# Running sums kept by columns in the scan turns by columns of a two-layer scan, attention and experts kernel

## The chip, the cores and the metric

The kernel runs on one core of one Trainium2 chip. A core has five engines, each with a queue of its own that is worked through in order: PE (TensorE, matrix products), DVE (VectorE), ACT (ScalarE), POOL (GpSimd) and SP (SyncE, which here starts nearly all transfers). PE's weight loads are shown as an engine of their own, PEld. The metric is the device time of one execution in microseconds (us); lower is better.

## What is computed

The input `x` is 4 images of 384 channels and 32 x 32 places, all in float32. Layer 0 normalizes it by groups and runs a selective scan over the 1024 places of each image in four directions `k`: by rows, by columns, and both of these backwards. Layer 1 is attention with a causal window of 64 and six heads, and then a mixture of four experts of which each token uses two. Cut to what the change touches:

```python
def _cross_scan(x):
    x0 = x.reshape(B, D, H * W)
    x1 = jnp.transpose(x, (0, 1, 3, 2)).reshape(B, D, H * W)
    return jnp.stack([x0, x1, x0[..., ::-1], x1[..., ::-1]], axis=1)
...
def step(h, inp):
    dtt, ut, bt, ct = inp
    dA = jnp.exp(dtt[..., None] * A)
    h = h * dA + (dtt * ut)[..., None] * bt[:, :, None, :]
    y = jnp.einsum('bkdn,bkn->bkd', h, ct)
    return (h, y)
...
ys = ys + Ds.reshape(K, D)[None, :, :, None] * u
...
y0 = ys[:, 0]
y2 = ys[:, 2][..., ::-1]
yt = ys[:, 1] + ys[:, 3][..., ::-1]
yt = jnp.transpose(yt.reshape(B, D, W, H), (0, 1, 3, 2)).reshape(B, D, L)
return y0 + y2 + yt
```

The state has 16 numbers for each channel and place; `y` sums over them. The results of the four directions and the term with `Ds` are added up place by place, and directions 1 and 3 come by columns and have to be turned for that.

## The kernel before

**How the order comes about.** The kernel's parts are generators. A recorder, `Machine` (line 213), runs them all against a model of the core: each step asks for one operation or, through `Engine.all` (144), for several at once; `Engine.ask` (155) gives it a price; `account` (264) adds the price to the engine's clock; `choose` (324) takes the one that can start first, moved by a bias. The experts have the bias `LATER`, +6 us, and most other parts `EARLY`, -6 us. The instructions go out in the order so found, on each engine. Prices are thus no times of the chip, but they set the order on all five queues. For a product on PE whose output has 32 partitions the price is that of line 180, and line 197 marks it as `steady`, which `account` (275) reads: other products take 1.9 times their price when the model thinks PE's clock is low, a steady one doesn't. `work` (198) is what the model counts as PE's activity for that.

**The scan.** A turn is one image `b` and one direction `k`; `ORDER` (538) puts the directions by columns, 1 and 3, ahead of 0 and 2, so turns 0, 1, 4, 5, 8, 9, 12 and 13 of the 16 go by columns. In a turn there are 12 blocks of 32 channels, and for each block four slots of four states; one slot fills a tile of 128 partitions (32 channels x 4 states) by 1024 places. For every slot:
- POOL multiplies the spread input by the spread `B` into a tile `z` (`times_b`, 801); there are seven tiles `z`.
- ACT makes the decay `dA` in PSUM (`decay`, 817); there are two of these.
- DVE scans (`scan`, 843), and POOL or DVE multiplies by the spread `C` (`times_c`, 830).
- PE adds the states up (`fold_y`, 873). Two blocks go together. Each of the two tiles `z` of a step is multiplied by `fold`, a 128 x 32 matrix that adds four partitions each, once for each half of the image's 32 rows. The four products write four groups of 32 partitions of one PSUM bank `ps`, 512 places wide. After four steps the bank holds the sums over all states, 16 products in all.

The sums over the directions run through memory. `normal` (659) writes `dsum` times the normalized input, `yd`, to `ydr`, as two halves of 512 places for each channel. `fold_y` loads the sums so far into `prev`, starts the bank with the product `ident` x `prev`, lets the sixteen products add to it, copies the bank back over `prev` on ACT (901) and stores it. Layer 1 reads `ydr` when an image is done, in `tile` (965). In all turns `ydr` lies by rows. A tile `z` of a turn by columns has its 1024 places as 32 columns of 32 rows, so its half is read as 16 rows by 32 columns, with steps of 32 elements:

```python
if k % 2:
    rhs = z.rearrange("p (w h) -> p h w", h=HH)[:, ts(h, HH // 2), :]
else:
    rhs = z[:, ts(h, LH)]
```

**Beside and after the scan.** `layer1` (1431) takes up an image when its four turns are done: attention in `tokens` (946), the choice of experts in `route` (1189). `experts` (1297) works on 19 blocks of 128 tokens for each image. For one block there are eight weight tiles of 576 KB, 36 products for the hidden layer (`ps_hid`, bank to `gelus` on ACT) and 12 for the output (`y_ff`). `combine` (1389) puts the results together. So layer 1 of one image runs beside the scan of the next ones, and that of the last image and what is left of the others comes after the last scan. ACT changes its function table (`ACT_TABLE_LOAD`) when it goes from the exponential to Gelu, to the logarithm or back.

Of the kernel before, what the change touches and what calls it, by code (L numbers as in the profile page):

```python
# [12 lines left out]
AF = mybir.ActivationFunctionType  # L13
# [5 lines left out]
B, D, HH, WW = 4, 384, 32, 32  # L19
# [52 lines left out]
class Stock:  # L72


    def __init__(self, m, pool, tag, n, shape):
        self.m, self.free = m, []
        self.tags, self.queue = {}, []
        self.add(pool, tag, n, shape)
# [32 lines left out]
class Op:  # L111


    def __init__(self, eng, outs, ins, cost, table, size):
        self.eng, self.outs, self.ins, self.cost, self.table, self.size = eng, outs, ins, cost, table, size
        self.work = 0.0
        self.steady = False


TABLES = {AF.Exp: "exp", AF.Ln: "ln", AF.Gelu: "gelu", AF.Sqrt: "sqrt"}  # L120
# [10 lines left out]
class Engine:  # L131
# [12 lines left out]
    def all(self, calls):  # L144

        asked = [self.ask(*c) for c in calls]
        outs, ins = ([ap for o in asked for ap in getattr(o, side)] for side in ("outs", "ins"))
        whole = Op(self.name, outs, ins, sum(o.cost for o in asked), None, 0)
        whole.work = sum(o.work for o in asked)
        whole.steady = asked[-1].steady  # L150
        yield whole
        for op, a, k in calls:
            getattr(self.real, op)(*a, **k)  # L153

    def ask(self, op, a, k):
        aps = [v for v in list(a) + [v for n, v in k.items() if n not in ("out", "accum_out")] if hasattr(v, "tensor")]
        if "out" in k:
            outs, ins = [k["out"]], aps
        else:
            outs, ins = aps[:1], aps[1:]  # L160
        if op == "value_load":
            outs, ins = [], aps
        if op == "tensor_tensor_reduce":
            outs, ins = outs + ins[-1:], ins[:-1]
        if k.get("accum_out") is not None:
            outs = outs + [k["accum_out"]]
        for v in list(k.values()):
            if isinstance(v, bass.IndirectOffsetOnAxis):
                ins = ins + [v.ap]
        n = max(v.free_size() if callable(v.free_size) else v.free_size for v in (outs if op == "matmul" else outs + ins))  # L170
        size, table = 0, None
        if "dma" in op:
            size = max(_nbytes(v) for v in outs + ins[:1])
            if op == "indirect_dma_start":
                size = P * D * 4
            cost = dict(pool=1.0, act=0.38, sp=0.48)[self.name]
        elif self.name == "pe":
            cost = max(n, 90) * (0.00088 if op == "transpose" else 0.00176)
            if outs[0].shape[0] == 32:
                cost = 0.108 + 0.000417 * n  # L180
            if ins[0].shape[0] < 32:
                cost *= 0.6
        elif self.name == "act":
            cost = 0.08 + 0.00085 * n + 0.1 * sum(hasattr(k.get(v), "tensor") for v in ("bias", "scale"))
            cost += 0.19 if "accum_out" in k else 0.0
            table = TABLES.get(a[2]) if op == "activation" else None
        elif self.name == "pool":
            cost = 0.1 + 0.0022 * n
        elif self.name == "sp":
            cost = 1.5  # L190
        else:
            cost = 0.17 + 0.00198 * n if "scan" in op else 0.14 + 0.00105 * n
            if n < 256 and not any(v.space == PSUM for v in outs + ins):
                cost += 0.5
        asked = Op(self.name, outs, ins, cost, table, size)
        if self.name == "pe":
            asked.steady = outs[0].shape[0] == 32
            asked.work = cost * min(ins[0].shape[0], P) / P if outs[0].shape[0] > 32 else 0.5 * cost
        return asked


def _nbytes(ap):
    n = 4
    for s in ap.shape:
        n *= s
    return n
# [6 lines left out]
class Machine:  # L213
# [50 lines left out]
    def account(self, op, start):  # L264
        e = op.eng
        if op.table and op.table != self.table:
            start += TABLE_LOAD
            self.table = op.table
        end = start + op.cost
        if e == "pe":  # L270

            left, end = op.cost, start
            while left > 0:
                n = int(end / WINDOW)
                f = 1.0 if op.steady or self.worked.get(n - 1, 0.0) > WINDOW / 3 else COLD
                step = min(left * f, (n + 1) * WINDOW - end + 1e-6)
                self.worked[n] = self.worked.get(n, 0.0) + op.work * step / f / op.cost
                left, end = left - step / f, end + step
        self.busy[e] += end - max(self.clock[e], start)
        self.clock[e] = end  # L280
        if op.size:
            self.dma = max(self.dma, end) + op.size / DMA_RATE
            end = max(end + DMA_TIME, self.dma + 1.0)
            e = "dma"
        for aps, log, w in ((op.ins, self.read, False), (op.outs, self.written, True)):
            for ap in aps:
                name = ap.tensor.name
                if str(ap.space) .endswith("DRAM"):
                    self.dram.setdefault(name, []).append((*self.span(ap), end, w))
                elif log.get(name, (0.0, None))[0] <= end:  # L290
                    log[name] = end, e
        self.reach = max(self.reach, end)
# [80 lines left out]
WINDOW, COLD = 3.413, 1.9  # L373
# [5 lines left out]
def conv_attn_hybrid(  # L379
# [35 lines left out]
    dsum = const.tile([P, T], F32, name="dsum")  # L415
# [58 lines left out]
    with tc.tile_pool(name="setup", bufs=1) as setup:  # L474
# [15 lines left out]
        for j in range(JB):  # L490
            ps = banks.now("ps_al")
# [44 lines left out]
    pwl = dram.tile([P, T * D], F32, name="pwl", bufs=1)  # L536

    ORDER = (1, 3, 0, 2)
    turns = [(b, ORDER[ki]) for b in range(B) for ki in range(KG)]
    blocks = [(i, t, j) for i in range(len(turns)) for t in range(T) for j in range(JB)]  # L540
    NSLOT = len(blocks) * NG
# [7 lines left out]
    pe, act, dve, pool, sp = m.pe, m.act, m.dve, m.pool, m.sp  # L549
# [65 lines left out]
    def group_norm(b):  # L615
# [21 lines left out]
        ps = yield from banks.take("ps_gm", 0)  # L637
# [21 lines left out]
        def normal(t):  # L659
            u = yield from us_.take("un")  # L660
            yield from sp.dma_start(u, x[b, ts(t, P)].rearrange("p h w -> p (h w)"))
            yield from act.activation(
                u, u, AF.Identity, bias=g_off[:, t : t + 1], scale=g_rstd[:, t : t + 1]
            )
            yield from sp.dma_start(udr[b][t], u)
            yd = yield from zs_.take("yd")
            yield from act.activation(yd, u, AF.Copy, scale=dsum[:, t : t + 1])
            us_.give(u)
            for j in range(JB):
                yield from sp.dma_start(  # L670
                    ydr[b][t, j].rearrange("(q d) l -> d q l", q=2),
                    yd[32 * j : 32 * j + 32, :].rearrange("d (q l) -> d q l", q=2),
                )
            zs_.give(yd)

        yield from m.together([normal(t) for t in range(T)], T if b == 0 else 1, EARLY)
        have.add(("u", b))

# [194 lines left out]
    def fold_y(n):  # L873


        i, t, j = blocks[n]
        b, k = turns[i]
        rows_y = ydr[b][t, j : j + 2].rearrange("j r l -> (j r) l")
        prev = yield from yps.take("yp")
        yield from sp.dma_start(prev, rows_y)  # L880
        ps = None
        for g in range(NG):
            s = n // 2 * SP + 2 * g
            yield lambda: s in ready and s + 1 in ready
            pair = zs[s], zs[s + 1]
            yield m.settled(*pair)
            mm = Calls()
            if ps is None:
                ps = yield from banks.take("ps_y", 0)
                mm.matmul(ps, ident, prev, start=True, stop=False)  # L890
            for n_z, z in enumerate(pair):
                for h in range(2):
                    if k % 2:
                        rhs = z.rearrange("p (w h) -> p h w", h=HH)[:, ts(h, HH // 2), :]
                    else:
                        rhs = z[:, ts(h, LH)]
                    q = 32 * (2 * n_z + h)
                    mm.matmul(ps[q : q + 32, :], fold, rhs, start=False, stop=g == NG - 1)
            yield from pe.all(mm)
            zs_.give(zs.pop(s), zs.pop(s + 1))  # L900
        yield from act.copy(prev, ps)
        banks.give(ps)
        yield from sp.dma_start(rows_y, prev)
        yps.give(prev)
        folded[b] = folded.get(b, 0) + 2
        if folded[b] == KG * NB:
            have.add(("scan", b))
# [601 lines left out]
```

## Time and profile before

| | before |
|---|---|
| median of 3 runs | 4246.56 us (4246.25 to 4254.88) |
| profiled execution, its own time | 4255.8 us |
| its span, first to last instruction | 4254.0 us |
| mean granted clock of PE | 0.819 |
| PE, PEld busy | 3377.0, 1952.7 us |
| DVE, ACT, POOL busy | 2852.8, 2373.1, 2813.7 us |
| `ps_y<-z,fold` on PE | 3072 records, 827.1 us busy |
| first and last of them | 112.6 and 3174.1 us |
| function table loads on ACT | 340 and 1 at the start, 1283 ns each |
| scan of the last turn's end to the end of all | 1079 us |

Busy time counts overlapping records once. A float32 product leaves two records on PE, so 3072 records are 1536 products. A record's length is not what a product costs when others run beside it: the four products of a step write different groups of partitions and overlap. What one costs is read from when the next starts. PE's granted clock is shown as a share of full speed. The turns start at about 113, 278, 441, 621 us (image 0), 776, 989, 1194, 1404 (image 1), 1590, 1777, 1985, 2190 (image 2) and 2397, 2599, 2794, 2992 us (image 3).

### The profile page before, as it was taken

The page shows a single profiled execution, that of the slowest core. Times are in us where ns is not written, and L with a number is a line of the kernel's source. Part 1 is how long each engine was busy: PE and PEld are TensorE (multiplying, and loading weights), DVE is VectorE, ACT ScalarE, POOL GpSimd, SP SyncE. Part 2 cuts the span into 40 slices and gives each one's busy share as a digit, 9 for nine tenths or more (in the row PEclk, how much of TensorE's full clock was granted, in tenths as well). Part 3 has the DMA queues.
Part 4 walks back from the last instruction along what each step waited for, and adds up shares of the span by engine and source line. Part 5 has one row for each costly group of instructions (what it writes and reads, how often), then busy time and mean ns, then how long its engine had stood idle before and what let it go on. Part 6 is the DMA issues. An engine that isn't in the chain of part 4 may idle for free. (4 is left out here: it accounts for less than half of the span.)

```text
span 4254.0 us, 50073 instructions
## 1 busy us (share of the span) xinstructions
PE 3377.0 (79%) x16222; PEld 1952.7 (46%) x16222; DVE 2852.8 (67%) x2995; ACT 2373.1 (56%) x3961; POOL 2813.7 (66%) x1468
## 2 busy tenths in 40 slices
PE   2556555588875987978788787887899999999997
PEld 1000110144441553534445343444567777887875
DVE  2999999987888978888888888888861222001001
ACT  2555455666655887777677767677663443222221
POOL 1999989997897899988878889898871001101001
PEclk7655665687875998878788887887899999999997
DMA  6566563542446985635668846556577438998995
GB/s 210 200 239 230 202 227 127 177 150 107 150 145 240 365 326 189 221 124 195 211 232 293 297 149 205 187 189 216 176 248 260 138 103 301 355 319 294 313 319 165
DMA packets 368573, 935.16 MB, mean 220 GB/s; under 512 B 48372, under 2 KB 160120, under 8 KB 368312
## 3 DMA queue, kind: packets, MB, share of 16 engines
q1 hardware_dynamic: 360120, 906.79, 61.3%
q0 software_dynamic: 8192, 25.17, 1.7%
q8 instruction: 129, 2.11, 0.2%
q14 instruction: 132, 1.08, 0.1%
HBM read 786.39 MB, written 164.30 MB: 223 GB/s over the span
## 5 line engine op out<-in xcount | busy, mean ns | idle before, releaser
L142 POOL TENSOR_TENSOR z<-dts,bc 128x1024 f32<-128x1024 f32 x768 | 1796.2, 2364 | 236.5 <-PE ps_y L153 136.9
L142 ACT ACTIVATE dA<-dts,a 128x1024 f32<-128x1024 f32 x768 | 853.1, 1118 | 488.6 <-DVE z L142 467.6
L153 PE MATMUL ps_y<-z,fold 128*32 128x512 f32 x3072 | 827.1, 914 | 320.8 <-DVE z L142 162.8
L142 DVE TENSOR_TENSOR_SCAN dA<-dA,z 128x1024 f32<-128x1024 f32 x414 | 947.3, 2288 | 111.1 <-ACT dA L142 92.1
L142 POOL TENSOR_TENSOR z<-z,bc 128x1024 f32<-128x1024 f32 x354 | 831.1, 2360 | 101.0 <-DVE z L142 100.1
L142 DVE TENSOR_TENSOR_SCAN z<-dA,z 128x1024 f32<-128x1024 f32 x354 | 795.7, 2276 | 55.7 <-ACT dA L142 53.1
L153 PEld LDWEIGHTS ps_hid<-xbt,w_sb 128*128 128x128 f32 x5472 | 683.4, 201 | 136.5 <-issue 22.4
L153 PE MATMUL ps_hid<-xbt,w_sb 128*128 128x128 f32 x5472 | 702.0, 286 | 40.7 <-ACT dt L142 16.4
L153 PE MATMUL y_ff<-w_sb,hs 128*128 128x384 f32 x1824 | 664.4, 503 | 14.3 <-ACT hs L142 7.9
L142 ACT ACTIVATE hs<-ps_hid,bb 128x128 f32<-128x128 f32 x912 | 271.9, 366 | 542.2 <-PE ps_hid L153 417.3
L142 DVE TENSOR_TENSOR z<-dA,bc 128x1024 f32<-128x1024 f32 x414 | 505.9, 1222 | 23.3 <-PE ps_y L153 0.5
L153 PEld LDWEIGHTS ps_y<-z,fold 128*32 128x32 f32 x3072 | 93.9, 122 | 800.7 <-POOL z L142 336.5
L142 ACT ACT_TABLE_LOAD x340 | 436.2, 1283 | 12.0 <-PE ps_g L153 5.8
L153 PEld LDWEIGHTS y_ff<-w_sb,hs 128*128 128x128 f32 x1824 | 333.4, 196 | 228.0 <-issue 40.3
L142 POOL DMA_INDIRECT cb<-ysdr,idx x64 | 61.8, 966 | 548.8 <-DMA cb<-t2dr 269.7
L153 POOL TENSOR_TENSOR rn<-rn,half 128x1 f32<-128x1 f32 x96 | 52.6, 548 | 288.6 <-DVE rn L153 286.6
L142 DVE COPY xbt<-ps_xb 128x384 f32<-128x384 f32 x40 | 22.2, 556 | 329.2 <-PE ps_xb L153 329.2
L153 PE MATMUL ps_y<-yp,ident 128*128 128x512 f32 x192 | 139.1, 814 | 90.0 <-ACT yp L142 20.9
L142 POOL DMA_INDIRECT xsdr<-tks,idx x64 | 63.7, 995 | 208.5 <-DMA xsdr<-tks,idx 151.3
L153 PE MATMUL ps_o<-v,pt 128*128 128x64 f32 x720 | 160.1, 345 | 6.1 <-ACT dt L142 2.3
L142 DVE COPY yb<-y_ff 128x384 f32<-128x384 f32 x27 | 15.0, 556 | 214.4 <-PE y_ff L153 205.1
L153 PEld LDWEIGHTS ps_o<-v,pt 128*128 128x128 f32 x720 | 130.1, 228 | 43.7 <-ACT dt L142 4.0
(187 smaller groups left out, 3480.3 us busy)
## 6 DMA issues: line engine op xcount, KB each, us to landing
w_sb<-wl SPq DMA_DIRECT2D x608, 576.0 KB
dts<-dtr SPq DMA_DIRECT2D x384, 512.0 KB
bc<-xdr SPq DMA_DIRECT2D x128, 512.0 KB
ub<-udr SPq DMA_DIRECT2D x48, 512.0 KB
dtr<-e SPq DMA_DIRECT2D x48, 512.0 KB
dtr<-dt SPq DMA_DIRECT2D x48, 512.0 KB
yp<-ydr SPq DMA_DIRECT2D x96, 256.0 KB
ydr<-yp SPq DMA_DIRECT2D x96, 256.0 KB
```

Of the source, the lines that this page charges most:

```text
L142: return getattr(self.real, op)(*a, **k)
L153: getattr(self.real, op)(*a, **k)
```

## The change

The sums in `ydr` lie by columns while the two turns by columns of an image run, and by rows from then on. `yd` is written in that layout (each half as 32 columns of 16 rows), so ACT reads `u` with steps of 32 elements. In the turns by columns PE reads the half of `z` as 32 columns of 16 rows, each column a run of 16 elements. In the second of these turns, direction 3, ACT's copy of the bank writes `prev` by rows, with steps of 32 elements. Sizes, products and transfers stay what they are.

Three things in the recorder change too. The price of a product with 32 output partitions goes from 0.108 + 0.000417 n to 0.01 + 0.00022 n. The mark `steady` is gone, so such a product too takes 1.9 times its price where the model thinks the clock is low. `Engine.all` hands on the function table of its operations.

```diff
@@ Engine.all
-        whole = Op(self.name, outs, ins, sum(o.cost for o in asked), None, 0)
+        table = next((o.table for o in asked if o.table), None)
+        whole = Op(self.name, outs, ins, sum(o.cost for o in asked), table, 0)
         whole.work = sum(o.work for o in asked)
-        whole.steady = asked[-1].steady
@@ Engine.ask
             if outs[0].shape[0] == 32:
-                cost = 0.108 + 0.000417 * n
+                cost = 0.01 + 0.00022 * n
...
         if self.name == "pe":
-            asked.steady = outs[0].shape[0] == 32
             asked.work = cost * min(ins[0].shape[0], P) / P if outs[0].shape[0] > 32 else 0.5 * cost
@@ Machine.account
-                f = 1.0 if op.steady or self.worked.get(n - 1, 0.0) > WINDOW / 3 else COLD
+                f = 1.0 if self.worked.get(n - 1, 0.0) > WINDOW / 3 else COLD
@@ conv_attn_hybrid
     ORDER = (1, 3, 0, 2)
+    LAST_BY_COLUMNS = 3
@@ normal
-            yield from act.activation(yd, u, AF.Copy, scale=dsum[:, t : t + 1])
+            yield from act.activation(
+                yd.rearrange("p (q w h) -> p q w h", q=2, w=WW),
+                u.rearrange("p (q h w) -> p q w h", q=2, w=WW), AF.Copy, scale=dsum[:, t : t + 1],
+            )
@@ fold_y
                     if k % 2:
-                        rhs = z.rearrange("p (w h) -> p h w", h=HH)[:, ts(h, HH // 2), :]
+                        rhs = z.rearrange("p (w h) -> p w h", h=HH)[:, :, ts(h, HH // 2)]
...
-        yield from act.copy(prev, ps)
+        if k == LAST_BY_COLUMNS:
+            yield from act.copy(
+                prev.rearrange("p (h w) -> p w h", w=WW), ps.rearrange("p (w h) -> p w h", w=WW)
+            )
+        else:
+            yield from act.copy(prev, ps)
```

## The prediction

> **What bounds the kernel now.** I read the page's busy shares, then windows on the work's stages, then PE's timeline, and the waits last. PE is busiest over the whole span, but that average mixes two stages: the scans end at 3174.6 us (last `ps_y<-z,fold`), and from there PE does little but the experts' two products. In the windows view (columns: stretch, length, busy us of PE, PEld, DVE, ACT and POOL, with counts, granted clock, DMA share, GB/s):
>
> ```profile
> 113.00:278.00 165.00, 97.22 (x234) 14.23 (x230) 159.38 (x107) 88.08 (x99) 154.70 (x68) 0.62 0.62 222
> 800.00:3175.00 2375.00, 1916.31 (x9013) 1060.01 (x9009) 2001.59 (x2024) 1678.29 (x2631) 2062.04 (x1038) 0.82 0.59 206
> 3175.00:4254.00 1079.00, 1037.97 (x6185) 819.79 (x6183) 150.69 (x464) 298.06 (x883) 91.51 (x126) 0.95 0.76 258
> ```
>
> The first scan turn is DVE's: 159 of 165 us busy, PE 97. From 800 us nothing is full (POOL 87%, DVE 84%, PE 81%, ACT 71%): the in-order queues wait on one another. The tail is PE's, 1038 of 1079 us. So time goes where PE has to do expert work after the last scan, and what PE does earlier shortens the tail. The tail's rate is in one undisturbed block of experts (four chunks of hidden and output products and one turn of the input):
>
> ```profile
> 3640.33:3656.44 16.11, 16.11 (x101) 12.93 (x100) 1.11 (x2) 3.53 (x12) 2.91 (x3) 1.00 1.03 403
> ```
>
> Now the sums that the change touches. First records in turn 5 (by columns, reading every 32nd element), then turn 7 (by rows), both at full clock, from PE's timeline:
>
> ```profile
> 989.47 1.90 PE L153 MATMUL ps_y<-z,fold 128*32 128x512 f32 x8
> 991.30 0.55 PE L153 MATMUL ps_g<-ident,yl 128*128 128x128 f32 x3
> ...
> 1434.46 1.92 PE L153 MATMUL ps_y<-z,fold 128*32 128x512 f32 x16
> 1436.31 0.59 PE L153 MATMUL y_ff<-w_sb,hs 128*128 128x384 f32 x1
> ```
>
> A group of four matmuls leaves 8 records (3072 for 1536 in the program). By columns one group holds PE until the next product starts, 991.30 - 989.47 = 1.83 us; by rows two take 1436.31 - 1434.46 = 1.85, so 0.93 each. The same by tile (min/median/max ns, whole turns 4 and 5, then 7):
>
> ```profile
> L153 PE MATMUL ps_y<-z,fold x384: 1024/1035/1206, 776.1 to 1185.3; 128*32 128x512 f32 x192
> ...
> L153 PE MATMUL ps_y<-z,fold x192: 592/593/1060, 1404.4 to 1579.7; 128*32 128x512 f32 x192
> ```
>
> At the low clock both take the same: in turn 3, by rows, half groups (the two matmuls of one `z`) take 1.92 us, as in turn 0, by columns:
>
> ```profile
> 645.50 1.92 PE L153 MATMUL ps_y<-z,fold 128*32 128x512 f32 x4 [1.79 <-DVE z L142]
> ...
> 264.39 1.92 PE L153 MATMUL ps_y<-z,fold 128*32 128x512 f32 x4 [2.69 <-POOL z L142]
> ```
>
> So a better read is worth about 0.9 us a group, and only at full clock.
>
> **What the Trainium skill says.** "SBUF — State Buffer", Specifications (TRN2): lines are 16 bytes, full bandwidth wants at least two hits on each, and each crossing pays. Elements 128 bytes apart hit a line once; the trace agrees (1035 against 593 ns). Runs of 16 f32 hit each line four times: by the page they read at full rate. No record of the kernel before shows such runs. "Advanced Engine Details and Errata", PSUM Cachelines, is gloomier: any access that isn't contiguous slows matmuls, though it then asks only for pairs; the output here stays contiguous. "TensorE: Matmul & The Clock Gate", What's actually happening: the clock is half or full, nothing between; so a mean clock c means a share 2c - 1 at full. The records' two levels, 593 and 1060, agree.
>
> **The change part by part.**
>
> *The read.* Only the turns by columns change. Turns 0 and 1 are DVE's and mostly at low clock: worth nothing, since DVE hides it. In turns 4, 5, 8, 9, 12, 13 the windows give clocks 0.74, 0.82, 0.87, 0.81, 0.81, 0.79; the shares at full clock are 0.48, 0.64, 0.74, 0.62, 0.62, 0.58, mean 0.61. Of 6 x 24 = 144 groups 88 gain 1.83 - 0.93 = 0.90 us: 79 us of PE. Bounds: 0 (the runs read like single elements) and 0.90 x 144 = 130 (all at full clock). I take the row rate, for the reason of the line size.
>
> *The recorder.* It writes the order on all engines by its own prices. A group of four at n = 512 was charged 4 x (0.108 + 0.2135) = 1.286 at any clock; now 4 x 0.1226 = 0.49, or 0.93 where it believes the clock low. (The table that `all` now hands on is always empty: only PE, DVE and POOL use `all`.) The program of after has the same work, moved: all four turns of batch 0 still hold no expert product on PE, and before the last `ps_y<-z,fold` stand 1,224 hidden matmuls in place of 1,017 and 399 output matmuls in place of 333. A block has 36 and 12: 207/36 = 5.75 and 66/12 = 5.5, so 5.6 blocks leave the tail, 5.6 x 16.11 = 90 us off it. That counts wholly, because PE is 96% busy there. The attention matmuls stand on the same side as before (432 `ps_qk` before the last fold in both).
>
> *What it costs in the scans.* PE gets 90 us more and 79 less: +11, at its busy share there (1916/2375 = 0.81) 14 us. If the queues absorb it in the 459 us PE now idles, 0; I take 14.
>
> *ACT.* In the order of turns 4 to 15, 316 table loads stand where 289 did: 27 x 1.283 (`ACT_TABLE_LOAD`) = 35 us. The copies that turn the sums (24) write every 32nd element; the nearest row is `xo<-ps_x`, 582 ns straight and 1119 at most with such a write: 24 x 0.54 = 13 us. Of the 12 `yd` copies, now read with such a step and in batches 1 to 3 nine, between 0 and 9 x 1.1 = 10 us (doubling 1143 ns). Some 57 us of ACT beside 697 us idle. DVE waited on ACT's `dA` 89.2 + 53.1 = 142 us in this stretch, so part arrives: a quarter, 15 us (0 to 57). The bank that a turned copy holds 0.5 us longer and the 3 `yd` copies before the first scan stay under 5 us in all and are inside this.
>
> *SP and DMA.* Counts are equal. The weights of 5.6 blocks (8 x 576 KB each, 26 MB) start in the scans: over 2375 us 11 GB/s on 206, hidden by a DMA share of 0.59. In turn 7, at 0.91 already, 27 more hidden matmuls are 0.75 block, 3.5 MB, at 403 GB/s 9 us if nothing hides it. I take 0. `dts` loads are queued on the same SP behind the weights; that is what would be late.
>
> Sum: -90 + 14 + 15 = -61 us. Against its own execution (4255.8, span 4254.0) 4195; on the median 4246.56, 4185.
>
> **Rivals.**
>
> *Runs of 16 read no faster (slower).* Place: the 88 groups at full clock. Then PE gets 90 us unpaid, 90/0.81 = 111 in the scans; and each group, charged 0.49 against 1.83, is 1.34 late where it was 0.55: 88 x 0.79 = 70, of which half passes to ACT and DVE, 35. -90 + 111 + 35 + 15 = +71: 4318. For it: the second page. Against: the line size. Between the two ends the result falls 132 us over 0.90 us, so 61 are used up 0.42 us above the row rate: it decides from about 1.35 us a group on.
>
> *The plan promises too much (no change).* The charge was near the mean (1.286 against 0.93 and 1.9), now it is half of either. In the six row turns clocks of 0.68, 0.93, 0.81, 0.89, 0.81, 0.88 give 96 groups at full clock and 48 at low: lateness before 48 x 0.63 = 30, after 96 x 0.44 + 48 x 0.99 = 90, so +60; by columns about +11. If all of these 71 us reach the scans: -61 + 71 = +10, 4257. For it: nothing on ACT can overtake a copy that waits for PE. Against: PE waits for `z` far more than `z` for PE: 336.5 + 317.9 us of its weight loads' waits, 137.1 the other way, so most lateness falls into gaps.
>
> *The scans get shorter too.* POOL waited on `ps_y` 24.1, 17.5 and 25.0 us in the three stretches by columns, and DVE 63.0 + 35.1 on `ps_o` and `ps_s` from 800 us on. Half of the first and a third of the second are 66: 4119. Against: row turns, with a fast sum, take as long (1189 us for six, 1210 by columns).
>
> **How the numbers follow.** The forecast, 4185, has 0.50, its own range 4130 to 4235 (0 or 57 on ACT, 9 on DMA, PE's saving up to 130). The shorter scans have 0.18, the overfull plan 0.15, the slow read 0.12, and 0.05 is for what I don't see in a new order on five queues, slower. The range 4105 to 4270 leaves out the slow read, half of the last and a little at the low end. 0.2% is 8.5 us, about the spread of the three runs and what can be told from no change. Faster: 0.50 + 0.18 and a third of 0.15, less a little, 0.72. Same: a third of 0.15, 0.06. Slower: the rest, 0.22.
>
> **What would show it.** A median near 593 ns for the folds in turn 8 shows the read right; 1035 shows it wrong. The last fold near 3174.6 + 29 and a tail near 990 us confirm the split; a tail 90 us shorter with a last fold past 3260 speaks for the overfull plan, with more waits of POOL and ACT on `ps_y`. The turned copies near 1.1 us and 363 table loads beside 340 show ACT's part. I am wrong if the tail keeps its 1079 us: then PE was not what it was made of.

## The result, and the profile after

| | before | after |
|---|---|---|
| median | 4250.72 us (4 runs, 4246.25 to 4264.91) | 4206.01 us (4 runs, 4193.36 to 4210.73) |
| ratio to before, 95% interval | | 0.9885 (0.985 to 0.9919) |
| span of the profiled execution | 4254.0 us | 4209.0 us |
| last fold starts (the 3174.1 given above is its weight load) | 3174.6 us | 3219.4 us |
| from there to the end | 1079 us | 990 us |
| PE busy | 3377.0 us | 3272.0 us |

The change makes the kernel faster by 1.15%. The split matters more than the sum: the tail is 90 us shorter and the scans are 45 us longer. The windows view of after, on the stretches that answer to those of before (columns: stretch, length, busy us of PE, PEld, DVE, ACT and POOL with counts, granted clock, DMA share, GB/s):

```profile
113.00:283.00 170.00, 93.13 (x236) 16.39 (x234) 163.20 (x109) 90.80 (x102) 161.01 (x72) 0.61 0.63 222
800.00:3221.00 2421.00, 1919.30 (x9574) 1132.96 (x9571) 2013.82 (x2051) 1749.33 (x2718) 2061.45 (x1045) 0.82 0.62 216
3221.00:4209.00 988.00, 949.89 (x5625) 751.86 (x5623) 139.83 (x442) 275.88 (x822) 85.06 (x118) 0.94 0.73 250
```

The first turn is DVE's as before. In the middle stretch PE has as much busy time as before (1919 against 1916 us) and has done 560 records more: what the folds gave up, expert products took. ACT is 71 us busier. The tail is still PE's, 96% busy.

The fold itself, from PE's timeline in turn 8, by columns, at full clock:

```profile
1612.31 1.06 PE L152 MATMUL ps_y<-z,fold 128*32 128x512 f32 x8
1613.31 2.27 PE L152 MATMUL ps_hid<-xbt,w_sb 128*128 128x128 f32 x18
```

A group holds PE for 1613.31 - 1612.31 = 1.00 us where 1.83 stood before. By tile, whole turns 8 and 9 (min/median/max ns):

```profile
L152 PE MATMUL ps_y<-z,fold x384: 592/617/1063, 1612.3 to 1995.6; 128*32 128x512 f32 x192
```

Median 617 ns, the row rate. Function table loads are 363 where 340 stood, and the turned copies take up to 1073 ns. Both lines are of after, from the page and from the tile view:

```profile
L141 ACT ACT_TABLE_LOAD x363 | 465.7, 1283 | 23.4 <-PE ps_g L152 9.6
```

```profile
L141 ACT COPY yp<-ps_y x96: 573/586/1073, 145.3 to 3220.6; 128x512 f32<-128x512 f32 x96
```

So every part of the change does what it says. The question left is why 75 to 80 us less of PE's work in the scans and 90 us less of tail come to 45.

### The profile page after: what moved, and what is told of

The parts are those of the page before. It is cut to its first block, busy times and chain, and to the rows that moved or that the text cites. A ratio compares the mean times of both kernels' runs of the same rounds, so it can differ in the third digit from the quotient of the medians.

```text
span 4209.0 us, 50108 instructions
## 1 busy us (share of the span) xinstructions
PE 3272.0 (78%) x16222; PEld 1959.0 (47%) x16222; DVE 2849.5 (68%) x2989; ACT 2428.8 (58%) x3984; POOL 2808.0 (67%) x1468
## 5 line engine op out<-in xcount | busy, mean ns | idle before, releaser
L152 PE MATMUL ps_y<-z,fold 128*32 128x512 f32 x3072 | 712.5, 787 | 386.3 <-POOL z L141 240.9
L152 PE MATMUL ps_dt<-xd,dtw_sb 12*128 12x512 f32 x192 | 97.9, 855 | 51.7 <-ACT dt L141 20.4
```

## The experiments

Ratios are to runs of before on the same chip. What decides is mostly one line: the tile view's row of all folds, whose last number is the start of the last one, the end of the scans. The tail is the span less that. A turn is counted from its first fold to the next turn's first.

A profile shows one execution, and those of one version lie up to 32 us apart (`rows_strided`, 4242.59 to 4274.52 us). The tails of the five versions that keep the order of after and all products after the scans (after, `prices_only`, `half_fold`, `rows_strided`, `relu_after`) lie within 4 us (986 to 990), so nearly all of that is in the scans. A difference of 10 or 20 us between two ends of scans can therefore be chance where the ratios of the medians don't show it too.

### The read alone, and the prices alone

The change has two parts that can be taken apart cleanly. The recorder's prices do not depend on how an operand is read, so with the old recorder the order on all queues is that of before, and with the new one that of after (in each pair the traces list the same sequence on PE, DVE, ACT and POOL). `read_only` is before with the layouts, the read and the turned copies. `prices_only` is before with the recorder's edits:

```diff
-                cost = 0.108 + 0.000417 * n
+                cost = 0.01 + 0.00022 * n
...
-                f = 1.0 if op.steady or self.worked.get(n - 1, 0.0) > WINDOW / 3 else COLD
+                f = 1.0 if self.worked.get(n - 1, 0.0) > WINDOW / 3 else COLD
```

> The sums by columns and the runs of 16, with the recorder of before: the order on every queue is that of before (1,017 hidden matmuls before the last fold). Theory A, the recorder pays: what PE is spared in the turns by columns (about 79 us) becomes waiting, the tail keeps its 1079 us, the scans end 0 to 30 us earlier: 4215 to 4250. Theory B, the read pays by itself because PE sets the pace of the turns by columns: scans end 60 or more earlier, 4190 or less.

> The recorder of after with the sums by rows and the read in steps of 32: the order of after, folds by columns at 1035 ns. Theory A: the tail is that of after (990 us), and without what the read spares PE the scans end 60 us or more later than in after: 4265 to 4320, slower than before. Theory B2, the read is worth nothing under this order since PE waits for z anyway: 4200 to 4220, as after.

The folds of before, then of `read_only`, `prices_only` and after:

```profile
L153 PE MATMUL ps_y<-z,fold x3072: 592/1035/1206, 112.6 to 3174.6; 128*32 128x512 f32 x192
```

```profile
L153 PE MATMUL ps_y<-z,fold x3072: 592/617/1064, 113.8 to 3158.8; 128*32 128x512 f32 x192
```

```profile
L153 PE MATMUL ps_y<-z,fold x3072: 592/1035/1204, 112.2 to 3241.0; 128*32 128x512 f32 x192
```

```profile
L152 PE MATMUL ps_y<-z,fold x3072: 592/617/1064, 113.8 to 3219.4; 128*32 128x512 f32 x192
```

| | order of before | order of after |
|---|---|---|
| read in steps of 32: scans end, tail | 3174.6, 1079 | 3241.0, 989 |
| read in runs of 16: scans end, tail | 3158.8, 1081 | 3219.4, 990 |
| ratio, steps of 32 | 1 | 0.9947 (0.9929 to 0.9966) |
| ratio, runs of 16 | 0.9968 (0.9949 to 0.9987) | 0.9885 (0.985 to 0.9919) |

Down the columns is the read: it ends the scans 16 us sooner in the old order and 22 in the new one; by the ratios of the medians it is 14 and 26 us. It spared PE 75 us of busy time in the old order, by the pages (the second is `read_only`):

```profile
PE 3377.0 (79%) x16222; PEld 1952.7 (46%) x16222; DVE 2852.8 (67%) x2995; ACT 2373.1 (56%) x3961; POOL 2813.7 (66%) x1468
```

```profile
PE 3302.4 (78%) x16222; PEld 1964.5 (46%) x16222; DVE 2851.1 (67%) x2995; ACT 2393.7 (56%) x3961; POOL 2808.1 (66%) x1468
```

So a fifth of the spared time arrived (in the new order 68 us were spared and 22 arrived, a third). Most was spared where it could count: 68 of the 75 us fall in the six turns by columns from turn 4 on, and these take 1189 us in place of 1209. There three tenths arrived, and four tenths in the new order (64 us and 25). The first four turns, which are DVE's, got no shorter. Theory A holds for the read. Across the rows is the order: 90 us of tail for 66 or 61 us of scans. For the prices both theories fail: `prices_only`, with the old slow read, is not slower than before, as A had it, but 0.5% faster, since its scans end only 22 us later than those of after; and its 4234.49 us are above the 4220 of B2. Both parts help alone; whether they help each other (0.85% as a sum, 1.15% together) is within the intervals.

### Is PE the pace of the scans?

`half_fold` spares PE more, `rows_strided` takes some back. The edits in `fold_y`, on after (in the first the price keeps n = 512):

```diff
 # half_fold
-                        rhs = z.rearrange("p (w h) -> p w h", h=HH)[:, :, ts(h, HH // 2)]
+                        rhs = z.rearrange("p (w h) -> p w h", h=HH)[:, : WW // 2, ts(h, HH // 2)]
...
-                        rhs = z[:, ts(h, LH)]
+                        rhs = z[:, h * LH : h * LH + LH // 2]
...
-                    mm.matmul(ps[q : q + 32, :], fold, rhs, start=False, stop=g == NG - 1)
+                    mm.matmul(ps[q : q + 32, : LH // 2], fold, rhs, start=False, stop=g == NG - 1)
 # rows_strided
-                        rhs = z[:, ts(h, LH)]
+                        rhs = z.rearrange("p (w h) -> p h w", h=HH)[:, ts(h, HH // 2), :]
```

> After with every fold 256 columns wide in place of 512, priced as before so that the order is that of after; half of the sums over states are left out. Spares PE some 0.46 us in each of about 200 groups at full clock and 0.9 in about 90 at the low one from turn 4 on: about 170 us, twice what the change spared. Theory A, PE does not set the pace of the scans and a fifth to a quarter of spared time arrives (the read: 16 to 21 of 79): scans end 30 to 50 us earlier than in after, about 4165. Theory B, PE sets the pace of the row turns: scans end 100 or more earlier, 4110 or less.

> After with the turns by rows reading z in steps of 32 elements, which puts their sums at other places; the order is that of after. Adds 0.9 us to about 110 groups at full clock in the six row turns, 100 us of PE. Theory A (a quarter arrives): row turns 1244 + 20 to 30, 4230. Theory B (PE sets the pace of the row turns, full of expert work): row turns 80 or more longer, 4290 or more.

```profile
L152 PE MATMUL ps_y<-z,fold x3072: 378/404/637, 114.2 to 3175.4; 128*32 128x256 f32 x192
```

```profile
L152 PE MATMUL ps_y<-z,fold x3072: 592/1035/1204, 113.9 to 3258.0; 128*32 128x512 f32 x192
```

`half_fold`, which leaves out half of the sums, has PE 3036.6 us busy, 235 less than after. Its scans end 44 us sooner (47 by the ratios), median 4160, ratio 0.9775 (0.974 to 0.9809). That is a fifth, but 103 of the 235 us fall in the first four turns, where they bring 5. From turn 4 on it is 128 us (170 were estimated) for 39, three tenths. `rows_strided` has PE 82 us busier; its scans end 39 us later, all in the row turns (1284 against 1243 us), ratio 0.9997 (0.9986 to 1.0009), which is 48 us by the ratios. That is a half, between the two theories: time given to PE in turns full of expert work seems to cost more than time taken from it brings. In no case does PE set the pace outright.

### What the moved expert work costs the scans

Four runs, in two pairs. Each pair makes one cut in after and in `read_only`, that is in both orders with the new read, whose scans end 61 us apart as they are. In the first pair the experts' Gelu is a Relu on the chip and priced as Gelu; in the second, a third of the experts' products are issued and priced as whole. The first puts another function in Gelu's place and the second leaves two thirds of the products out, so only their times are of use.

```diff
 # relu_after, relu_read_only
-                yield from act.activation(
-                    hs[:, ts(j, P)], ps[:, ts(j, P)], AF.Gelu, bias=bbs[o][:, jj : jj + 1]
-                )
+                arg, bias = (hs[:, ts(j, P)], ps[:, ts(j, P)]), dict(bias=bbs[o][:, jj : jj + 1])
+                yield act.ask("activation", (*arg, AF.Gelu), bias)
+                act.real.activation(*arg, AF.Relu, **bias)
 # lite_after, lite_read_only: hidden; output likewise, with j == 0 alone
+                            if t == 0:
+                                one.matmul(
+                                    ps[:, ts(j, P)], w[:, j * P : j * P + P], xts[o][:, :P],
+                                    start=True, stop=True,
+                                )
-                    yield from pe.all(mm)
+                    yield from pe.all(mm, one)
```

> After with the experts' Gelu replaced by Relu on the chip alone, priced as Gelu: the same order, 215 table loads of 1283 ns fewer in all, 206 of them (264 us of ACT) in turns 4 to 15. If ACT's loads are what the moved expert work costs the scans, the scans end 100 us or more earlier than in after, and the gap of its scans to those of the next kernel (62 us with Gelu) falls below 25. If PE or the expert work itself is, the gap stays 45 to 70.

> The same replacement in the kernel with the new read and the order of before. Its scans end some 60 us (gap as with Gelu) or under 25 us (gap made by table loads) ahead of those of relu_after. Tail near 1080 less what ACT's loads delay in it, 0 to 20.

> After with a third of the experts' products (one of three partial sums of the hidden and of the output layer; the other two are left out), priced as whole, so the order on every queue is that of after; weights, Gelu, table loads and copies stay. Theory A: what moved expert work costs the scans is its PE time in PE's queue; then the gap between the scans of this one and of the next (62 us with whole experts) falls to a third, 20 us or so, and both scans end 100 us or more earlier. Theory B: it is the rest (Gelu on ACT, weights, the order on the other queues); then the gap stays at 45 or more.

> The same cut in the kernel with the new read and the order of before. Its scans end 20 us (A) or 45 us and more (B) ahead of those of lite_after.

| | scans end, new order | scans end, old order | gap |
|---|---|---|---|
| whole | 3219.4 | 3158.8 | 60.6 |
| Relu | 3205.8 | 3136.5 | 69.3 |
| a third of the experts' products | 3189.5 | 3145.8 | 43.7 |

```profile
L141 ACT ACT_TABLE_LOAD x148 | 189.9, 1283 | 24.2 <-PE ps_g L152 20.7
```

The page of `relu_after` shows the loads gone (148 for 363). Taking 264 us off ACT in turns 4 to 15 brought 14 us, which can be chance; in the old order 219 brought 22. That is a twentieth to a tenth. The gap stays. So table loads are not what the new order costs.

The folds of `lite_after`, then of `lite_read_only`:

```profile
L152 PE MATMUL ps_y<-z,fold x3072: 592/906/1063, 112.7 to 3189.5; 128*32 128x512 f32 x192
```

```profile
L153 PE MATMUL ps_y<-z,fold x3072: 592/861/1063, 113.3 to 3145.8; 128*32 128x512 f32 x192
```

Of the gap, 17 us go with two thirds of the experts' products. The other 44 stay, just under the 45 that were named for theory B. Theory A is missed in both its parts: the gap is not 20, and the scans end 30 and 13 us sooner, not 100. For that PE's busy time in turns 4 to 15 fell by 216 and 170 us. (Its granted clock fell too, from 0.82 to 0.75 and from 0.80 to 0.74, and the median record of the folds rose from 617 ns to 906 and 861, so the gain is smaller than the cut alone would give.)

The 44 us lie in the row turns: 1227 us against 1183 in this pair, while the turns by columns take 1182 and 1183. With whole products it is the same, and that is telling: of the 207 hidden products that the new order moves ahead (half the records of `ps_hid` on PE, counted by turn), 126 go into the turns by columns, which are 4 us longer (1193 against 1189), and 81 into the row turns, which are 52 us longer (1243 against 1191). Where most of the work went it cost nothing that can be seen.

The waits say only in part why. Summed over the six row turns, from the waits view of each (us):

| | POOL, for PE to be done with a tile `z` | DVE, for ACT | row turns |
|---|---|---|---|
| `read_only`, after | 68, 99 | 77, 90 | 1191, 1243 |
| `relu_read_only`, `relu_after` | 57, 87 | 61, 74 | 1174, 1225 |
| `lite_read_only`, `lite_after` | 75, 75 | 75, 102 | 1183, 1227 |

With whole products the new order makes POOL wait longer for PE. With a third of them it doesn't, DVE waits longer for ACT instead, and most of the gap is still there. So neither queue alone carries it. Late transfers of the scan's input, which the prediction feared, are not the cause: POOL waits for `dts` once, 69.2 us in after and 69.7 in `read_only`.

### The price of a fold

Three versions of after, each with one number changed in the recorder:

```diff
-                cost = 0.01 + 0.00022 * n
+                cost = 0.01 + 0.000435 * n      # price_as_measured
+                cost = 0.01 + 0.00005 * n       # price_lower
...
-EARLY, LATER = -6.0, 6.0
+EARLY, LATER = -6.0, 2.0                        # experts_sooner
```

> After with a fold priced at what it costs on the chip (0.01 + 0.000435 n, 0.93 us a group of four). The order holds 999 hidden matmuls before the last fold where after has 1,224. If the low price of after is what made the row turns longer (lateness of PE), the scans end 60 us or more before those of after, at 3160 or less, and the total is 4200 or less in spite of a tail about 95 us longer (1085). If the row turns are longer only because they hold more expert work, the total is that of before less a little: 4215 to 4255.

> After with a still lower price of a fold (0.01 + 0.00005 n): the order holds 1,278 hidden matmuls before the last fold, 54 more than after, 1.5 blocks, 24 us off the tail. At 0.7 us of scan for each us moved 17 of them come back: 7 us faster than after, 4199. If lateness from the wrong price counts, 4210 or more.

> After with the bias LATER at +2 in place of +6: 1,260 hidden matmuls before the last fold, one block more than after. By 0.7 us of scan for each us moved 5 us faster than after, 4201; if experts that stand closer to the folds hold up the scans, later than after, 4215.

The folds of the three, in that order:

```profile
L152 PE MATMUL ps_y<-z,fold x3072: 592/617/1063, 114.8 to 3137.0; 128*32 128x512 f32 x192
```

```profile
L152 PE MATMUL ps_y<-z,fold x3072: 592/617/1064, 114.5 to 3276.7; 128*32 128x512 f32 x192
```

```profile
L152 PE MATMUL ps_y<-z,fold x3072: 592/617/1063, 114.5 to 3217.2; 128*32 128x512 f32 x192
```

| | price of a group, us | hidden products before the last fold | scans end | tail | ratio |
|---|---|---|---|---|---|
| `read_only` | 1.29 | 1,017 | 3158.8 | 1081 | 0.9968 (0.9949 to 0.9987) |
| `price_as_measured` | 0.93 | 999 | 3137.0 | 1095 | 0.9949 (0.9932 to 0.9966) |
| after | 0.49 | 1,224 | 3219.4 | 990 | 0.9885 (0.985 to 0.9919) |
| `price_lower` | 0.14 | 1,278 | 3276.7 | 970 | 0.9951 (0.9937 to 0.9966) |
| `experts_sooner` | 0.49 | 1,260 | 3217.2 | 966 | 0.9862 (0.983 to 0.9894) |

The prices are those at what the model takes for the full clock; all but that of `read_only` are 1.9 times as high where it thinks the clock low. The true price gives the shortest scans of the five, 82 us shorter than after, and loses because it leaves 225 hidden products more to the tail. So the first theory's scans came (3160 or less) with the second one's total (4215 to 4255; the median is 4237.98). A price far too low gives 57 us longer scans for 20 us of tail; that is much more than the 0.7 us for each us moved that was expected of it. (Its profile is of an execution of 4248 us, where the median is 4236.) And with the price of after, `experts_sooner` puts one block more into the scans at no cost that can be seen: they end 2 us sooner and the tail is 23 us shorter. Even in the row turns alone, 927 hidden products take 1229 us there and 873 take 1243 in after; that may be chance, but it is no sign of a cost. So it is not the amount of expert work that stretches the scans, or not alone. The order that follows from the price does; whether because PE is then late is not shown, since every price moves the experts as well. Nor was the mark `steady` tried by itself. Of the versions that leave nothing out `experts_sooner` is the fastest, 4191.66 us where 4201 or 4215 were expected, but its interval overlaps that of after.

### How long a run has to be

`read_only` with another run length for each image, the rest of its order and prices the same:

```diff
-                        rhs = z.rearrange("p (w h) -> p w h", h=HH)[:, :, ts(h, HH // 2)]
+                        run = (16, 2, 4, 8)[b]
+                        rhs = z[:, ts(h, LH)].rearrange("p (a c r) -> p c a r", r=run, c=32 // run)
```

> As the first of these, but the turns by columns of image 1 read z in runs of 2, those of image 2 in runs of 4, those of image 3 in runs of 8 elements, each run 32 elements from the next; image 0 keeps 16. Which places a sum belongs to changes with it, so the sums of images 1 to 3 by columns are of other places. If a line of 16 bytes must be hit twice, all four read at the row rate (median near 600 ns at full clock). If each line costs something, runs of 2 and 4 stay nearer 1035.

From the tile view, images 1, 2 and 3 (runs of 2, 4 and 8), the turns by columns:

```profile
L153 PE MATMUL ps_y<-z,fold x384: 592/776/1062, 779.0 to 1180.8; 128*32 128x512 f32 x192
...
L153 PE MATMUL ps_y<-z,fold x384: 592/617/1062, 1586.4 to 1963.8; 128*32 128x512 f32 x192
...
L153 PE MATMUL ps_y<-z,fold x384: 592/617/1062, 2387.8 to 2767.8; 128*32 128x512 f32 x192
```

and from the timeline a group at full clock with runs of 2, then of 4:

```profile
987.72 1.33 PE L153 MATMUL ps_y<-z,fold 128*32 128x512 f32 x8
988.99 0.55 PE L153 MATMUL ps_g<-ident,yl 128*128 128x128 f32 x3
...
1586.41 1.07 PE L153 MATMUL ps_y<-z,fold 128*32 128x512 f32 x8
1587.40 0.91 PE L153 MATMUL y_ff<-w_sb,hs 128*128 128x384 f32 x2
```

A group takes 1.83 us with single elements, 1.27 with runs of 2, 0.99 with runs of 4, and no less with 16 (1.00). Neither expectation fits all lengths: runs of 4 reach the row rate, runs of 2 come two thirds of the way. Four float32, 16 bytes, are enough.

## Why the prediction was right, point by point

**The read: right.** It was put at 0.90 us for each of 88 groups, 79 us of PE. The group went from 1.83 to 1.00 and PE's busy time fell by 75 us with the order held, 68 of them in the six turns meant. The line size that "SBUF — State Buffer", Specifications (TRN2), gives fits: from runs of 4 on, which fill its 16 bytes, nothing more is gained. That two hits on a line give full bandwidth is not what runs of 2 show.

**The tail: right.** 5.6 blocks at 16.11 us were 90; it shrank from 1079 to 990. That it fits to the microsecond is luck: by the same rule the tails of `price_as_measured`, `price_lower` and `experts_sooner` should differ from that of after by +101, -24 and -16 us, and they differ by +105, -20 and -23.

**PE in the scans: the term of 14 us was mis-sized, and in two ways that nearly cancel.** It set 90 us of expert work against 79 us of folds, one for one, and divided by PE's busy share. Neither counts so. What the folds spare arrives at a fifth to a third (16 of 75, 22 of 68, 44 of 235), or three to four tenths of what falls in turns 4 to 15. At that busy share the 79 us would have been worth 97; they were worth 16 to 22. The 90 us of expert work would have cost 111; the new order costs 61 to 66. Together that is +45 with ACT's part in it, where 14 + 15 = 29 stood. This is the 16 us by which the sum missed (-45 in the spans against -61). That it missed by no more is luck: each of the two terms was off by 45 us or more.

**ACT: too dear.** A quarter of 57 us was counted as 15. The pair with Relu shows a twentieth to a tenth of ACT's time arriving, which would be 3 to 6 us for these 57. The size of ACT's additions was about right: 23 loads more in all, turned copies up to 1073 ns, `yd` at 2050 ns.

**The slow read as the rival that ends slower: wrong.** `prices_only` is that case, but for the strided copies, put at 23 of the 57 us of ACT. It takes 0.9947 of before, not 4318 us. The formula gave PE's time in the scans its full weight twice, as work and as lateness. With it the point from which a slow read would decide, 1.35 us a group, has no ground.

**The overfull plan: right in place, its mechanism not shown.** The stretch is in the row turns, as it said (1243 against 1189 us). Taken as all that the order costs, its 71 us are near the 61 to 66 measured; as an addition to 14 and 15 they were too much, since the kernel is clearly faster. Its mechanism is a charge at half the true time that makes PE late. For it speak the prices: the true one ends the scans 82 us sooner, a still lower one 57 later. But no run changed the price and kept the experts' place. POOL, which has to have a tile `z` back from PE, did wait longer for it, in the waits view of `read_only` and then of after:

```profile
POOL z L142 <- PE ps_y L153: 119.8, 55, 6.8
```

```profile
POOL z L141 <- PE ps_y L152: 164.3, 64, 11.9
```

Yet in `experts_sooner` it waits still longer and the scans are no longer than those of after:

```profile
POOL z L141 <- PE ps_y L152: 188.8, 64, 9.8
```

And in the pair with a third of the experts' products the row turns' waits for PE are equal, 75 us each, and 44 us of stretch remain. So lateness of PE is at most a part of it, and what the rest comes from stays open.

**The shorter scans: not seen.** The turns by columns take 1193 us in place of 1209, about the read's own share; nothing follows in the others.

## What to carry to other kernels

Time that one engine is spared counts where that engine sets the end. Here 75 us of PE, spared where the queues wait on one another, were worth 16, while moving 90 us of the same engine's work out of the stretch that it fills brought all 90, and cost two thirds of that where it was put. Nor is one engine's time alike throughout: 128 us less of folds in turns 4 to 15 made them 39 us shorter, 216 us less of experts' products 27, though both lowered the clock and neither figure is exact. When a change alters both an operation and the model that schedules it, build the two halves by themselves before saying which one pays: here the prices alone gave as much as the better read. And a scheduler's price can be wrong in the useful direction: the true price of a fold made the shortest scans of five plans and a slower kernel than after, because the price also decides how much other work is let in.

## What the runs showed of the hardware

- PE's moving operand in float32, rows 128 bytes apart at full clock: runs of 1, 2, 4 and 16 elements cost 1.83, 1.27, 0.99 and 1.00 us for a group of four products. At the low clock half a group took 1.92 us both by rows and with runs of 1.
- ACT pays for steps of 128 bytes on either side. `yd`, read so from SBUF, went from 1145 to 2050 ns for 1024 elements; the copy from PSUM that writes so took up to 1073 ns where 585 stood, for 512. Before, then after (the copy's line of after is shown above):

```profile
L142 ACT ACTIVATE yd<-un,dsum x12: 1131/1145/1162, 31.0 to 2111.2; 128x1024 f32<-128x1024 f32 x12
L142 ACT COPY yp<-ps_y x96: 557/585/627, 140.0 to 3175.2; 128x512 f32<-128x512 f32 x96
```

```profile
L141 ACT ACTIVATE yd<-un,dsum x12: 2003/2050/2104, 30.9 to 2133.2; 128x1024 f32<-128x1024 f32 x12
```
